# A tick's loads stand in the program behind its two sets, in place of ahead of them

## The chip, the core and the metric

The kernel runs on one core of a Trainium2 chip. The metric is device time in microseconds (us) of one execution. The program is written in Python and unrolled completely: every engine (PE for matmuls with PEld for its weight loads, DVE, ACT, POOL, and SP, which only issues DMAs here) gets its own list of instructions and works through it in the order in which the source emits them. A last pass (`keep_order`) ties each instruction to the one before it on its engine, so that the order of the source is the order of execution on every engine.

## What is computed

The input x is 8 images of 8 channels, 512 x 512, float32. Layer 0 normalizes groups of two channels and adds a spectral convolution of 4 x 4 modes. Layer 1 normalizes again (its result is called xn here) and then does this:

```python
drive = grid = xn
for _ in range(15):
    mapped = R * grid * (1.0 - grid)
    local = conv3x3_per_channel(mapped, K_local)
    grid = (1 - BETA) * ((1 - EPS) * mapped + EPS * local) + BETA * drive
cml = clip(grid, 0.0001, 1 - 0.0001)
nca = sigmoid(conv1x1(relu(conv3x3(xn, Wp, bp)), Wu, bu))        # 128 hidden channels
g = sigmoid(conv1x1(relu(conv3x3(concat(xn, cml, nca), Wg1, bg1)), Wg2, bg2))
out = x + g * cml + (1 - g) * nca
```

## The kernel before

**Elements and halves.** An element is one image (b = 0 to 7). The fifteen steps of an element are done in two halves of four channels each. A half keeps its grid in 5 tiles `m[k]` (k = 0 to 4), each of which holds four slabs of 32 rows. One *set* is one step of one tile: 96 matmul instructions into two PSUM pairs (`convolve`, L528), two DVE instructions that add the drive (`settle`, L583), and two squares on ACT (L589). A half has 75 sets, in the order of steps, and within a step of k. The drive comes in two layouts, dE for even steps and dO for odd ones, so a half needs 5 dE and 5 dO tiles as well.

**Ticks.** A tick, counted by t, does two sets, then up to two *hidden rounds* (L628 and the ReLU on ACT at L634 and on DVE at L636), then a gate or a piece of layer 0 of the next element, and, behind every second round, the 1 x 1 convolution of the hidden rounds (L647). An element has 75 ticks: its first half begins at t = 0, its second in the middle of tick 37. The hidden convolution of the next element and the gates of the previous element run beside the sets.

**Slots.** Work tiles live in slots. A `Slots` object is a first-in-first-out queue of free slots: `take` takes the one that came free first, `drop` appends one. A tile that is put into a slot waits, on the chip, for the last user of the tile that was there. `sets` has 15 slots, exactly what one half needs (5 m, 5 dE, 5 dO). The slots of dE and dO are dropped in `settle` at steps 14 and 15. The slot of m is dropped behind the store of its final grid (`leave`, the cml stores of L569), which is put off to the end of the tick. `shared` has 5 slots for gates (gin and mix, two slots a gate) and for the x tiles of layer 0.

**What a tick emits, in order.**
- `others.feed(t)`: loads of gates (six DMAs each, L683 and L688), when slots are free and at most one is loaded already; loads of x (L186). They go to SP.
- `prepare(n)` of each half in progress: n is the number of sets since that half's start, negative before it. For tile k, at n = k - 2 it takes a slot for m[k], POOL sets its edges (L507), and ACT squares dE into it (`square`, L508); at n = 2k - 5 POOL scales dO (`drive`, L521). From n = -11 on it also loads the half's dE and dO (four DMAs of 256 KB each, L491), as long as slots are free; also on SP.
- the two sets; between them `others.finish()`: the last DVE step of a gate (L726) and its out store (L733, on SP).
- the hidden rounds, with the load of the next cols tile behind every fourth (L611, on SP).
- the gate or layer 0 work; a gate is convolved (L698) in a later tick than the one in which it is loaded.
- `tick()`: what was put off. That is the exchange of halo rows between the m tiles (`renew`, L558), the cml stores (L569), the y store (L663), the store of xn (L417).

Before the first element come 8 rounds without sets, and behind the last one a tail that has only hidden rounds and gates; both go through the same `work`.

The lines that move:

```python
            while n >= -11 and self.loads and (self.loads[0][2] or sets.free):
                self.load(nc.sync)
```

## Time and profile before

| | |
|---|---|
| median of 3 runs | 10126.7 us (10123.93 to 10132.92) |
| the profiled execution | 10129.58 us, its span 10127.8 us |
| PE busy | 9436.5 us, 93% of the span |
| PEld, DVE, ACT, POOL busy | 4308.9, 5848.6, 4299.5, 1766.8 us |
| mean granted TensorE clock | 0.983 |
| moved by DMA | 1353.5 MB, 134 GB/s on average |

The span is the time from the first to the last instruction in one profiled execution. Busy times add up the instructions of an engine. In the lists of waits, "A <- B" means that A stood idle until B ended; "SPq" is the SP queue, and "issue" is idle time for which no semaphore is seen. In a timeline the columns are start in us, length in us, the engine and line, the operation, what it writes and reads, and how many were merged.

### The profile page before, as it was taken

What the parts mean: (1) busy time and instruction counts of PE and PEld (TensorE: products, weight loads), DVE (VectorE), ACT (ScalarE), POOL (GpSimd) and SP (SyncE); (2) the same over time, 40 slices, a digit from 0 to 9 for tenths busy, and PEclk for the clock granted to TensorE, in tenths of its full rate; (3) what the DMA queues carried; (4) which work ended last, traced back from release to release, by engine and by line L of the source; (5) the groups of instructions that cost most, each with busy time, mean ns of one, the idle gap of its engine ahead of it and who ended that gap; (6) DMA issues with size and microseconds to landing.
All of it is one profiled execution on the core that took longest, in us unless ns stands there. A gap on an engine that the chain in (4) does not pass through costs nothing. (4 is left out here: it accounts for less than half of the span.)

```text
span 10127.8 us, 353307 instructions
## 1 busy us (share of the span) xinstructions
PE 9436.5 (93%) x160496; PEld 4308.9 (43%) x160496; DVE 5848.6 (58%) x6067; ACT 4299.5 (42%) x4445; POOL 1766.8 (17%) x1406
## 2 busy tenths in 40 slices
PE   6998999999999999999999999999999999998999
PEld 3444444444444444444444444444444444444333
DVE  5654555755557555665555655566555665555555
ACT  2444444444444444444444444444444444444433
POOL 2010111202112021111211112111121201312212
PEclk9999999999999999999999999999999999999999
DMA  5231255535555465544555455554555535663578
GB/s 170 81 84 48 62 147 137 152 103 141 142 149 147 109 150 135 153 138 121 142 137 147 127 123 144 138 141 129 134 146 134 157 117 132 155 145 95 139 194 199
DMA packets 625565, 1353.50 MB, mean 134 GB/s; under 512 B 73067, under 2 KB 73195, under 8 KB 594051
## 3 DMA queue, kind: packets, MB, share of 16 engines
q1 hardware_dynamic: 621728, 1329.77, 50.7%
q8 instruction: 1261, 20.66, 0.9%
q14 instruction: 238, 1.94, 0.1%
q10 hardware_dynamic: 2338, 1.13, 0.0%
HBM read 992.27 MB, written 268.78 MB: 125 GB/s over the span
## 5 line engine op out<-in xcount | busy, mean ns | idle before, releaser
L528 PE MATMUL pair<-m,band 32*32 32x512 f32 x115200 | 4118.2, 608 | 177.2 <-issue 109.1
L589 ACT ACTIVATE m<-m 128x1024 f32<-128x1024 f32 x2240 | 2360.0, 1055 | 2811.5 <-DVE m L583 2695.1
L528 PEld LDWEIGHTS pair<-m,band 32*32 32x32 f32 x115200 | 2268.6, 104 | 1943.4 <-issue 1106.4
L628 PE MATMUL pair<-cols,w_p 32*128 32x511 f32 (+1 forms) x24576 | 2874.7, 605 | 42.8 <-issue 22.2
L583 DVE SCALAR_TENSOR_TENSOR m<-pair,dO 128x1024 f32<-128x1024 f32 x1280 | 1507.5, 1219 | 1372.5 <-PE pair L528 1176.3
L583 DVE SCALAR_TENSOR_TENSOR m<-pair,dE 128x1024 f32<-128x1024 f32 x1120 | 1319.7, 1220 | 1222.4 <-PE pair L528 1039.2
L628 PEld LDWEIGHTS pair<-cols,w_p 32*128 32x128 f32 x24576 | 1284.6, 187 | 1647.0 <-issue 1138.0
L636 DVE TENSOR_SCALAR h<-pair,b_p 128x1024 f32<-128x1024 f32 x1024 | 1313.5, 1283 | 838.7 <-PE pair L628 838.2
L634 ACT ACTIVATE h<-pair,b_p 128x1024 f32<-128x1024 f32 x1024 | 1140.7, 1114 | 990.0 <-PE pair L628 981.7
L721 POOL TENSOR_TENSOR mix<-mix 96x512 f32<-96x512 f32 x344 | 437.5, 1272 | 4413.2 <-ACT mix L719 4067.7
L647 PE MATMUL pair<-h,w_u 128*32 128x512 f32 x8192 | 1014.9, 606 | 205.4 <-DVE h L636 189.3
L698 PE MATMUL pair<-gin,w_g 128*32 128x511 f32 (+1 forms) x8256 | 965.7, 599 | 5.9 <-DMA mix<-xn 3.3
L703 POOL TENSOR_TENSOR mix<-mix 96x512 f32<-96x512 f32 x344 | 437.9, 1273 | 1420.7 <-DMA mix<-nca 1340.7
L593 POOL TENSOR_SCALAR dO<-dO 128x2048 f32<-128x2048 f32 x80 | 431.7, 5408 | 1263.2 <-DVE m L583 1263.1
L647 PEld LDWEIGHTS pair<-h,w_u 128*32 128x32 f32 x8192 | 254.3, 110 | 848.8 <-issue 367.6
L660 ACT ACTIVATE y<-y,b_u 128x512 f32<-128x512 f32 x256 | 184.8, 722 | 908.4 <-DVE y L656 908.4
L698 PEld LDWEIGHTS pair<-gin,w_g 128*32 128x32 f32 x8256 | 237.2, 110 | 681.6 <-issue 464.8
L715 PE MATMUL pair<-mix,w_g 128*32 128x512 f32 x2064 | 358.8, 595 | 85.2 <-DVE mix L708 85.2
L654 ACT COPY y<-pair 128x512 f32<-128x512 f32 x256 | 149.9, 585 | 631.1 <-PE pair L647 527.0
L708 DVE TENSOR_SCALAR mix<-pair,b_g 128x512 f32<-128x512 f32 x344 | 257.9, 750 | 254.2 <-PE pair L698 254.2
L726 DVE SCALAR_TENSOR_TENSOR mix<-mix,back 96x512 f32<-96x512 f32 x344 | 316.1, 919 | 150.8 <-POOL mix L721 150.8
L521 POOL TENSOR_SCALAR dO<-dO,base 128x512 f32<-128x512 f32 x320 | 226.8, 724 | 783.0 <-DMA dO<-xn 728.0
(85 smaller groups left out, 2642.2 us busy)
## 6 DMA issues: line engine op xcount, KB each, us to landing
gin<-xn SPq DMA_DIRECT2D x344, 384.0 KB
cols<-xn SPq DMA_DIRECT2D x256, 512.0 KB
x<-in_x SPq DMA_DIRECT2D x120, 1024.0 KB
gin<-cml SPq DMA_DIRECT2D x344, 320.0 KB
gin<-nca SPq DMA_DIRECT2D x344, 320.0 KB
dE<-xn SPq DMA_DIRECT2D x320, 256.0 KB
dO<-xn SPq DMA_DIRECT2D x320, 256.0 KB
mix<-xn SPq DMA_DIRECT2D x344, 192.0 KB
```

Source lines behind the costliest of these rows:

```text
L528: nc.tensor.matmul(ps[h // 2][32 * t : 32 * t + 32, h % 2], band[at, c0 + (t if step % 2 else h), dx], m[at, t, dx : dx + N], start=(n == ...
L583: nc.vector.scalar_tensor_tensor(u[:, at], ps[q], FLOOR, d[:, at], ALU.max, ALU.add)
L589: nc.scalar.square(u[:, at], u[:, at])
L593: nc.gpsimd.tensor_scalar(d, d, 0.5, None, ALU.add)
L628: nc.tensor.matmul(ps[g // 2][:, g % 2, lo:hi], w_p[p, dx, i % 2], self.cols[p, i // 2, at : at + hi - lo], start=(n == 0), stop=(n == 2), ...
L634: nc.scalar.activation(h[:, :2], ps[0], AF.Relu, bias=b_p)
L636: nc.vector.tensor_scalar(h[:, 2:], ps[1], b_p, 0.0, ALU.add, ALU.max)
L647: nc.tensor.matmul(ps[32 * g : 32 * g + 32], w_u[:, r % 4], h[:, g], start=(r == self.hs[0][0]), stop=(r == self.hs[-1][0]), tile_position ...
L698: nc.tensor.matmul(ps[32 * j : 32 * j + 32, lo:hi], gband[:, dx], gin[:, j, at : at + hi - lo], start=(n == 0), stop=(n == 2), tile_positi ...
L703: nc.gpsimd.tensor_tensor(d, d, ng, ALU.subtract)
L715: nc.tensor.matmul(ps[at], gpoint[:, at], mix[:, 3], start=True, stop=True, tile_position=(0, 32 * j),)
L721: nc.gpsimd.tensor_tensor(d, d, mix[: GR * C, 2], ALU.mult)
```

## The change

The loading loop leaves `prepare` and becomes a function of its own, `fetch`. A tick gathers its `feed` and the `fetch` of its halves in `transfers`, which `work` calls behind the two sets and behind `others.finish()`, ahead of the hidden rounds. The squares and drives of `prepare` stay where they were. The rounds ahead of the first element and the tail call theirs at the same place in `work`.

```diff
                 if 2 * k - 5 in (n, n + 1):
                     self.drive(k, 1)
+
+        def fetch(self, n):
             while n >= -11 and self.loads and (self.loads[0][2] or sets.free):
                 self.load(nc.sync)
...
-    def work(sets, rounds, e, after):
+    def work(sets, rounds, e, after, transfers):
...
         others.finish()
+        transfers()
         for ps in (pairs[:2], pairs[2:])[:rounds]:
             e.hidden.round(ps, after, settled)
...
-        work([], 2, e, None)
+        work([], 2, e, None, lambda: e.first.fetch(-11))
...
-            others.feed(t)
-            e.first.prepare(2 * t)
-            e.second.prepare(2 * t - TICKS)
+            halves = [(e.first, 2 * t), (e.second, 2 * t - TICKS)]
             if after:
-                after.first.prepare(2 * t - 2 * TICKS)
+                halves.append((after.first, 2 * t - 2 * TICKS))
+            for half, n in halves:
+                half.prepare(n)
+
+            def transfers():
+                others.feed(t)
+                for half, n in halves:
+                    half.fetch(n)
+
...
-            work(now_sets, min(more, 2 - e.hidden.n % 2), e, after and after.hidden)
+            work(now_sets, min(more, 2 - e.hidden.n % 2), e, after and after.hidden, transfers)
...
-        others.feed(TICKS)
-        work([], min(2, ROUNDS - e.hidden.n), e, None)
+        work([], min(2, ROUNDS - e.hidden.n), e, None, lambda: others.feed(TICKS))
```

## The prediction

> **What bounds the kernel now.** I read the page's busy shares and DMA queues (packets, MB, share), then the waits (us in total, times, longest us), then the timelines of single ticks.

> ```profile
> PE 9436.5 (93%) x160496; PEld 4308.9 (43%) x160496; DVE 5848.6 (58%) x6067; ACT 4299.5 (42%) x4445; POOL 1766.8 (17%) x1406
> q8 instruction: 1261, 20.66, 0.9%
> ```

> ```profile
> PE pair L528 <- issue: 109.1, 65, 4.5
> POOL m L507 <- DMA cml<-m: 114.2, 12, 16.5
> ACT m L508 <- POOL m L507: 44.2, 10, 12.4
> SPq L491 <- DMA cml<-m: 47.3, 51, 2.4
> ```

> TensorE is busy for 93% of the span, and no wait of PE names a load for more than 14.2 us in total. So a load's place can matter in two ways only: it makes TensorE wait through another engine, or it slows TensorE's own instruction stream. The four waits show both. "issue" is a PE gap that no semaphore explains. The next two are the squares (L508) that wait for a memset (L507), which waits until the store of a finished set has freed its slot. The last is the same wait, borne by the SP queue for loads, where it costs nothing.

> Where a square has this wait, this follows (timeline of ACT and POOL, then windows of three ticks; columns are length, PE, PEld, DVE, ACT, POOL busy, then the clock):

> ```profile
> 775.01 0.11 POOL L507 MEMSET m<- 128x8 f32 x1 [16.55 <-DMA cml<-m]
> 775.16 2.00 ACT L508 ACTIVATE m<-dE,mhalf 128x2048 f32<-128x2048 f32 x1 [9.72 <-POOL m L507]
> 777.06 2.93 ACT L589 ACTIVATE m<-m 128x1024 f32<-128x1024 f32 x3
> 779.90 1.09 ACT L634 ACTIVATE h<-pair,b_p 128x1024 f32<-128x1024 f32 x1
> ...
> 746.30:762.00 15.70, 14.22 (x264) 6.85 (x264) 8.41 (x7) 8.61 (x7) 8.79 (x11) 1.00 0.91 252
> 762.00:784.90 22.90, 16.40 (x266) 5.82 (x265) 7.97 (x7) 10.40 (x9) 9.89 (x9) 0.83 0.56 144
> ```

> The squares of the sets and the hidden rounds' L634 stand behind L508 on ACT; PE's L647 needs L634. The tick takes 22.9 us in place of 15.7, and the clock falls to 0.83.

> [...] 17% of 22.9 us = 3.9 us lost to the clock behind a 6.4 us gap. [...] 322,961 PE records / 256 = 1261.6, and q8 has 1261 packets. [...] every issue gap over 1 us ends at a record whose number has the same remainder by 256 (193), and a q8 packet began 2.2 to 3.2 us earlier. [...] the trace shows fetches 3 to 6 us late while gate loads are outstanding and within 1.5 us when nothing is.

> **The change, part by part.**

> Instructions: none is added or removed. All that is moved are DMA issues on SP (gate loads L683 and L688, x loads L186, set loads L491); feed and fetch issue nothing on other engines. Squares, memsets and drives stay at the head. In the SP queue the loads pass only the out store (L733) of the same tick; the cols loads, renewals (L558) and cml stores (L569) stay behind them.

> (a) Gate and x loads, later. A typical tick starts at 5318.5:

> ```profile
> 5320.57 0.38 SPq L663 DMA_DIRECT2D nca<-y  x1
> 5321.05 0.38 SPq L683 DMA_DIRECT2D gin<-xn  x1
> ...
> 5324.33 0.42 SPq L688 DMA_DIRECT2D mix<-nca  x1
> 5324.96 0.85 SPq L733 DMA_DIRECT2D out<-mix  x1
> ```

> The out store waits for DVE's L726 and goes out 6.45 us into the tick in nearly every gate tick. The six loads will follow it, at 7.3 to 10 in place of 2.5 to 6, about 5 us later on average. The gate's convolution comes in the next tick; from the landing of gin (judged by the queue's later waits) to L698 there are 18 us in the median now, so this costs nothing but some 8 us in the last element, whose ticks are 11 to 14 us and whose renewals have 2 to 12 us of slack. In the tail the last gates' loads stand behind an out store: 3 us.

> (b) A gain from the same shift. The sets occupy PE for the first 6.6 us of a tick, where 256 instructions pass in 4.4 us; behind them they take 8 to 11. So only a fetch asked for in the first 3 us stalls PE, and the gate loads go out just then. Issue gaps sum to 133 us (all lines), 85 of them in ticks with gate loads. About 20 of these are in ticks without an out store (the two-gate starts, t = 2 and 51), where nothing moves. Of the other 65 I take half as gained, 33: the shifted loads land until 18 us, that is, into the head of the next tick. Clock lost behind such gaps is 0.6 us for 1 us of gap (32 windows of 3.4 us at half speed behind 92 us of gaps), 20 more. The bounds are 0 and 104. In the hand-over ticks (c) the loads leave the head too: 10.

> (c) Slots handed over at a half's end. This is the largest part, and it is a matter of which slot goes to whom. Free slots form a queue. At the end of a half the slots of dE and dO come free in settle, those of m only after their cml store. Now a tick's squares are served first, from what earlier ticks freed. They take the d slots (the waits of L507 for "DVE m L583", 61 times), and the loads take the m slots and wait on SP. Only the fifth square of each half gets an m slot: the 12 waits above. With fetch behind the sets, the loads take the d slots in the tick that frees them. The next tick's squares find m slots alone. By hand, with n counted to the new half's start, and a slot named by the set of the old half (0 to 74) that frees it (m70 is the grid of set 70, d70 its drive): second halves give square 0 slot m70 (tick n = -3), squares 1 and 2 m72 and m73 (n = -1), square 3 d74, square 4 m74; first halves give squares 0 and 1 m71 and m72 (n = -2), squares 2 and 3 d74 and m73. The stores of m72 and m73 were issued at the end of the tick just before. So **a wait moves from SP to POOL and ACT**.

> Its price in a second half (SP timeline; the tick with n = -1 starts at 6879.9):

> ```profile
> 6864.59 1.77 SPq L491 DMA_DIRECT2D dO<-xn  x4
> 6866.40 1.85 SPq L491 DMA_DIRECT2D dE<-xn  x4
> 6868.76 4.08 SPq L491 DMA_DIRECT2D dO<-xn  x4
> 6873.73 8.08 SPq L569 DMA_DIRECT2D cml<-m  x8
> 6883.89 2.44 SPq L491 DMA_DIRECT2D dE<-xn  x4
> 6886.51 1.70 SPq L491 DMA_DIRECT2D dO<-xn  x4
> ```

> The last two loads show when the stores of m72 and m73 have landed: 6883.9 and 6886.5. The twelve loads ahead of the stores start at 6864.6 now. In the new order the first of them takes m71's slot, and m71's store itself stands behind eight loads that leave 5 us later. I reckon the first load at 6872, so the stores land 7 to 8 us later, the last at 6894.5. Then: square 2.0, L589 1.06, L634 1.11, L589 1.05, L634 1.11 = 6900.8; PE is at L647 at 6894.3 now: 6.5 lost. In the other five of elements 1 to 6 the store lands 0.6 to 4.6 us later in its tick; the six sum to 49. Element 0 (m73 lands at 760.5, L647 at 760.1): 14. Element 7 (m73 at about 9215.8): 18. Square 0 in the short ticks of elements 0 and 7: 9.

> First halves, seven: m72 lands at 4996.5 in the tick from 4986.6; no L589 stands between, so 4996.5 + 6 + 2.0 + 2.2 = 5006.7 against L647 at 5001.5: 5.2 each, 36.

> Clock: 15 gaps of 5 to 18 us at about 3 us: 45. Given back: the fifth square's store no longer stands behind loads: 7 in element 0, 12 in element 7, 1 in the others: 25. Sum: 49 + 14 + 18 + 9 + 36 + 45 - 25 = 146. Bounds: with no later landing the gaps of first halves vanish and 10 to 20 stays; with 3 us more it is 200.

> **Sum.** 146 + 8 + 3 - 33 - 20 - 10 = +94. The profiled execution took 10129.6 (span 10127.8), so 10223.6 by its own time; it stands 2.9 above the median, so 10221.

> **Rivals.**

> Faster: the fetches decide. The store of m72 lands no later than now (the DMA queue drains faster than I reckon), L508 then ends before L634 is due, and (b) brings its full 104 + 10. Against it: the 12 waits already there cost 7 us in element 0. Price: 20 + 11 - 114 = -83, 10044. It decides where the landing slips by less than about 3 us, half of what I reckon. Chance 0.10.

> No change: slip and fetches cancel, or SP trails so far that the loads' place is idle (in the tick from 5015.5 the gate loads already go out 6.5 us in). 10127. Chance 0.10.

> Slower, more: the shifted loads also push renewals and gate loads past their use in the last element's short ticks, 10 ticks by 4 us: 10261. Chance 0.12. My forecast has 0.68.

> So faster 0.10, within 0.2% (some 20 us, about what a measurement of this kernel can tell from no change) 0.10, slower 0.80. The range 10120 to 10285 takes in the cancelling case and the dearer one, and leaves the faster one out.

> **What would show it.** Right: the waits of L507 for cml stores rise from 12 to some 60 and those of L508 for L507 to over 150 us; "PE L647 <- ACT h L634" grows from 14 us to about 100, at 15 hand-overs; gate loads follow the out store; PE's issue gaps fall to about 90. Wrong: L508 without waits, or issue gaps near 20 with an unchanged L647.

## The result, and the profile after

The changed kernel takes 10068.3 us (median of 5 runs, 10056.9 to 10083.9), the kernel before 10126.7 us beside it. The ratio is 0.9947, 95% interval 0.9934 to 0.996: **faster by 0.5%**, where the prediction had it slower by 0.9%. The profiled execution has a span of 10066.0 us in place of 10127.8, so 61.8 us are to be found in the trace.

In the changed kernel's line numbers everything from `fetch` on stands two further down (L530 for L528, L509 and L510 for the memset and the square, L636 for L634). The page's lines of TensorE and the instruction queue, then rows of the waits (us in total, times, longest us), two of before and four of after:

```profile
PE 9398.8 (93%) x160496; PEld 4288.8 (43%) x160496; DVE 5870.8 (58%) x6067; ACT 4301.6 (43%) x4445; POOL 1764.5 (18%) x1406
q8 instruction: 1261, 20.66, 0.9%
```

```profile
PE pair L628 <- issue: 22.2, 16, 4.1
PE pair L647 <- ACT h L634: 14.2, 32, 6.4
```

```profile
PE pair L530 <- issue: 87.8, 65, 3.9
PE pair L649 <- ACT h L636: 23.8, 35, 9.8
POOL m L509 <- DMA cml<-m: 330.1, 27, 16.1
ACT m L510 <- POOL m L509: 116.0, 27, 15.3
```

The same work is done by the same number of instructions. The waits of the squares have grown as forecast: those of the memset for a store from 114 to 330 us, those of the square for the memset from 44 to 116. What did not come is their price: TensorE's wait for L636 grows by 10 us, from 14.2 to 23.8, not to about 100. And TensorE's unexplained gaps shrink: within the ticks they sum to 132.9 us before and 96.9 after.

**One tick shows where the time came from.** It is tick 58 of element 4. Its TensorE before, then after (start, length, instructions, and in brackets the idle time before them with what ended it):

```profile
5970.14 6.51 PE L528 MATMUL pair<-m,band 32*32 32x512 f32 x185
5979.80 1.93 PE L528 MATMUL pair<-m,band 32*32 32x512 f32 x7 [3.15 <-issue]
5981.66 7.44 PE L628 MATMUL pair<-cols,w_p 32*128 32x512 f32 x48
```

```profile
5918.05 6.58 PE L530 MATMUL pair<-m,band 32*32 32x512 f32 x192
5924.56 5.43 PE L630 MATMUL pair<-cols,w_p 32*128 32x512 f32 x48
```

Before, TensorE stops 7 instructions short of the sets' end, waits 3.15 us for no semaphore, and goes on slowly: the hidden rounds take 7.44 us in place of 5.43. SP's queue in the same tick, before and after (of six gate loads, the first and the last):

```profile
5968.82 0.35 SPq L683 DMA_DIRECT2D gin<-xn  x1
...
5970.96 0.42 SPq L688 DMA_DIRECT2D mix<-nca  x1
5976.58 0.86 SPq L733 DMA_DIRECT2D out<-mix  x1
```

```profile
5924.50 0.83 SPq L735 DMA_DIRECT2D out<-mix  x1
5925.44 0.82 SPq L685 DMA_DIRECT2D gin<-xn  x1
...
5928.10 0.92 SPq L690 DMA_DIRECT2D mix<-nca  x1
```

Before, six loads (1600 KB) go out around the tick's start; after, they follow the out store, 7.4 to 10 us into the tick. The windows of this tick, before and after (columns as in the prediction):

```profile
5970.14:5994.31 24.17, 21.02 (x290) 8.50 (x287) 10.03 (x10) 7.03 (x7) 2.51 (x2) 0.86 0.40 96
```

```profile
5918.05:5935.20 17.15, 17.15 (x290) 7.76 (x287) 10.03 (x10) 7.03 (x7) 2.56 (x2) 1.00 0.61 128
```

The same 290 matmuls and the same work on DVE and ACT take 24.17 us before and 17.15 after: 3.15 us of stall and 14% of the clock, 3.4 us, make 6.5 of the 7.0.

**The whole span, by kind of tick.** Each cell is the sum of tick lengths and, behind the stroke, of TensorE's issue gaps over 0.15 us, worked out from the traces. Gate ticks are t = 2 to 26 and 51 to 72 of elements 1 to 6; the hand-overs are t = 73 to 1 (second half to the next element's first) and t = 34 to 39 (first half to second).

| us / us of issue gaps | ticks | before | after | difference |
|---|---|---|---|---|
| gate ticks | 282 | 4778.9 / 83.1 | 4681.9 / 37.4 | -97.0 |
| hand-over second to first | 28 | 390.8 / 9.0 | 419.6 / 18.3 | +28.8 |
| hand-over first to second | 48 | 803.0 / 28.2 | 785.4 / 19.1 | -17.6 |
| rest of element 7 | 66 | 811.9 / 8.1 | 835.1 / 19.9 | +23.2 |
| rest of element 0, other ticks | 175 | 2676.8 / 4.5 | 2673.7 / 2.3 | -3.1 |
| ahead of the first tick, and tail | | 666.4 | 670.4 | +3.9 |

Clock lost in gate ticks falls from 46.1 to 10.2 us. With the 45.7 us of gaps that makes 81.6 of the 97.0; the other 15 are in neither. So the gain is larger than the result shows: what the hand-overs from second to first half and element 7 lose, 52 us, is over half of what the gate ticks gain.

### The profile page after: what moved, and what is told of

It is laid out like the page before. It is cut to its first block, busy times and chain, and to the rows that moved or that the text cites. A ratio compares the mean times of both kernels' runs of the same rounds, so it can differ in the third digit from the quotient of the medians.

```text
span 10066.0 us, 353339 instructions
## 1 busy us (share of the span) xinstructions
PE 9398.8 (93%) x160496; PEld 4288.8 (43%) x160496; DVE 5870.8 (58%) x6067; ACT 4301.6 (43%) x4445; POOL 1764.5 (18%) x1406
## 3 DMA queue, kind: packets, MB, share of 16 engines
q8 instruction: 1261, 20.66, 0.9%
## 5 line engine op out<-in xcount | busy, mean ns | idle before, releaser
L530 PE MATMUL pair<-m,band 32*32 32x512 f32 x115200 | 4123.9, 609 | 158.6 <-issue 87.8
L530 PEld LDWEIGHTS pair<-m,band 32*32 32x32 f32 x115200 | 2264.3, 104 | 1936.8 <-issue 1125.0
L630 PE MATMUL pair<-cols,w_p 32*128 32x511 f32 (+1 forms) x24576 | 2841.0, 601 | 30.4 <-DMA cols<-xn 14.4
L638 DVE TENSOR_SCALAR h<-pair,b_p 128x1024 f32<-128x1024 f32 x1024 | 1313.4, 1283 | 788.1 <-PE pair L630 787.1
L636 ACT ACTIVATE h<-pair,b_p 128x1024 f32<-128x1024 f32 x1024 | 1141.4, 1115 | 888.1 <-PE pair L630 875.0
L700 PE MATMUL pair<-gin,w_g 128*32 128x511 f32 (+1 forms) x8256 | 960.4, 598 | 9.5 <-DMA gin<-nca 3.6
L700 PEld LDWEIGHTS pair<-gin,w_g 128*32 128x32 f32 x8256 | 234.6, 109 | 683.8 <-issue 466.5
L728 DVE SCALAR_TENSOR_TENSOR mix<-mix,back 96x512 f32<-96x512 f32 x344 | 334.0, 971 | 150.8 <-POOL mix L723 150.8
L721 ACT ACTIVATE mix<-pair,b_g 96x512 f32<-96x512 f32 x344 | 233.0, 677 | 278.1 <-PE pair L717 184.0
```

The source lines that it names most:

```text
L530: nc.tensor.matmul(ps[h // 2][32 * t : 32 * t + 32, h % 2], band[at, c0 + (t if step % 2 else h), dx], m[at, t, dx : dx + N], start=(n == ...
L630: nc.tensor.matmul(ps[g // 2][:, g % 2, lo:hi], w_p[p, dx, i % 2], self.cols[p, i // 2, at : at + hi - lo], start=(n == 0), stop=(n == 2), ...
L636: nc.scalar.activation(h[:, :2], ps[0], AF.Relu, bias=b_p)
L638: nc.vector.tensor_scalar(h[:, 2:], ps[1], b_p, 0.0, ALU.add, ALU.max)
L700: nc.tensor.matmul(ps[32 * j : 32 * j + 32, lo:hi], gband[:, dx], gin[:, j, at : at + hi - lo], start=(n == 0), stop=(n == 2), tile_positi ...
```

## The experiments

Theory F: the gain is TensorE's instruction fetch (the packets of q8), and what counts is which DMAs are outstanding (issued and not yet landed) in the first microseconds of a tick. Theory S: it comes from the set loads and their slots. Theory Q: from the order in SP's queue. All ratios are against the kernel before on the same chip.

**Gate and x loads alone.** The set loads go back ahead of the sets (in this run and in those built on it, the loads of the opening go back to the head of their rounds too):

```diff
                 half.prepare(n)
+                half.fetch(n)
 
             def transfers():
                 others.feed(t)
-                for half, n in halves:
-                    half.fetch(n)
```

> The gate and x loads stand behind the two sets as in the changed kernel; the loads of dE and dO stay ahead of them as in the kernel before. Theory F (the gain is TensorE's instruction fetch, which no longer meets gate loads in the head of a tick): the gate ticks of elements 1 to 6 (t = 2 to 26 and 51 to 72) shorten as in the changed kernel, by 80 to 97 us, with their issue gaps near 37 us in place of 83; the hand-over from second to first half (t = 73 to 1) keeps the 391 us of before in place of 420; in all 10030 to 10060 us, faster than the changed kernel. Theory S (the gain comes from the set loads and the slots that they take): no change against before, 10120 to 10135, issue gaps in gate ticks near 80.

Measured: 10056.7 us, ratio 0.9938 (0.9925 to 0.9951). Gate ticks 4678.9 us with 37.1 us of issue gaps; the hand-over is back at 391.9. Moving the gate loads alone brings the whole gain. By the intervals it can't be told from the changed kernel, so that part of the expectation stays open; its profiled span, 10046.9 us, is 19 us shorter, but it is the fastest of its five runs.

**Set loads alone.** The mirror image:

```diff
+            others.feed(t)
             for half, n in halves:
                 half.prepare(n)
 
             def transfers():
-                others.feed(t)
                 for half, n in halves:
                     half.fetch(n)
```

> Only the loads of dE and dO stand behind the sets; gate and x loads stay ahead of them. Theory F: gate ticks keep their issue gaps (about 83 us) and length (4779 us); the hand-overs from second to first half take 415 to 425 us in place of 391, those from first to second 785 to 803; in all 10125 to 10160 us, not faster than before. Theory S: 10060 to 10080 us, the changed kernel's time.

Measured: 10138.4 us, ratio 1.0016 (1.0008 to 1.0025). Gate ticks 4782.8 / 90.5; hand-over second to first 424.5, first to second 788.1. Theory S falls: this half of the change costs 13 us by the medians, 8 to 25 by the interval.

**The gate loads later still**: the kernel with the gate loads alone moved, and these behind the hidden rounds:

```diff
         others.finish()
-        transfers()
         for ps in (pairs[:2], pairs[2:])[:rounds]:
             e.hidden.round(ps, after, settled)
         next(settled, None)
+        transfers()
```

> As with the gate loads alone moved, but they stand behind the hidden rounds too, so that they go out at 13 us of a tick or later and are outstanding in the first 5 us of the next. Theory F: it is not being behind the sets that counts but what is outstanding in the first 3 us of a tick: issue gaps in the gate ticks return to 70 us or more, time 10090 to 10170. Rival theory Q (the gain is SP's queue, in which something else had stood behind the gate loads): as fast as with the gate loads behind the sets, issue gaps near 37.

Measured: 10215.3 us, ratio 1.0091 (1.0074 to 1.0107), beyond the expected range. A wait of TensorE and a tick's SP queue (this tick starts at 5317.54 and ends at 5334.68):

```profile
PE pair L530 <- issue: 157.6, 105, 3.9
```

```profile
5329.56 0.39 SPq L613 DMA_DIRECT2D cols<-xn  x1
5330.05 0.41 SPq L685 DMA_DIRECT2D gin<-xn  x1
...
5332.51 0.42 SPq L690 DMA_DIRECT2D mix<-nca  x1
```

The loads leave 12.5 to 15 us into this tick, the last of them 2.2 us before the next begins. From the mean rate of this run's span, 133 GB/s, I estimate 12 us for their 1600 KB, so they are still under way in the next head. Gate ticks take 4829.9 us with 103.0 of issue gaps, more than before. So "later" is no gain in itself: of the three places, only 7.4 to 9.8 us into a tick (the median with these loads right behind the sets) has gained.

**Between the two sets**, ahead of the out store; otherwise as with the gate loads alone moved:

```diff
             next(settled)
+            if transfers:
+                transfers()
+            transfers = None
             others.finish()
         others.finish()
-        transfers()
+        if transfers:
+            transfers()
```

> The kernel with the gate loads alone moved, but they stand between the two sets, ahead of the out store (L733). SP runs ahead of TensorE, so without the out store's wait in front of them the loads should go out in the first 6 us of a tick as in the kernel before. Theory F: what counts is the time at which they go out, so issue gaps in gate ticks near 83 us and 10110 to 10145 us. Rival theory P (any place behind the first set will do): issue gaps under 50, time under 10080.

Measured: 10129.5 us, ratio 1.0004 (0.9992 to 1.0016); gate ticks 4789.0 / 91.4. The SP queue around a tick that starts at 5292.94:

```profile
5291.97 0.64 SPq L690 DMA_DIRECT2D mix<-nca  x1
5299.38 0.86 SPq L735 DMA_DIRECT2D out<-mix  x1
```

The loads stand behind a set in the program and yet go out ahead of it. In gate ticks the first and the last of them leave 2.5 and 5.3 us into a tick in the median, the same as in the kernel before (7.4 and 9.8 with the gate loads behind both sets), and nothing is gained. SP sent these loads as early as its waits let it. It is the out store's wait for DVE (in the changed kernel 273 waits of L735 for L728, 1482.5 us) that puts the loads behind the sets in time as well.

**Other traffic.** To the kernel with the gate loads alone moved are added six idle DMAs of 256 KB. In the program they stand at the head of the tick after each gate load:

```diff
                 g.load()
+                self.extra += 1
...
+            for i in range(6 * others.extra):
+                nc.sync.dma_start(
+                    out=view(spare[i % 12], 0, [[N, P], [1, N]]),
+                    in_=view(e.xn, 16 * i * C * N, [[N, P], [1, N]]),
+                )
+            others.extra = 0
```

> The kernel with the gate loads alone behind the sets, plus six idle DMAs of 256 KB each (from xn to a spare place in HBM that nobody reads) at the head of the tick after each gate load. Theory F: whatever moves in the first 3 us of a tick makes the fetch late: issue gaps in gate ticks go from 37 us back to 75 us or more, gate ticks from 4679 to 4750 or more, time 10110 to 10250, with no wait of PE for a DMA grown by more than 10 us. Rival theory Q (it was the place of the gate loads in SP's queue): issue gaps stay under 50 and the time within 20 us of 10057.

Measured: 10516.9 us, ratio 1.0385 (1.0368 to 1.0402): 460 us above the kernel without them, where at most 193 were expected. Its waits of TensorE:

```profile
PE pair L530 <- issue: 217.1, 117, 4.5
...
PE pair L700 <- DMA gin<-nca: 105.9, 33, 9.3
```

Issue gaps in gate ticks go from 37 to 196 us, and the clock lost there from 6.8 to 97.3. Of the 336 us that gate ticks grow by, the gaps are 158 and the clock 90. The second row was not expected: the traffic also delays gate loads, mostly in element 7.

The figures contradict Q, which had under 50 us of gaps. But the run is not the clean case that was meant. The idle DMAs did not keep to the head, and the gate loads kept their place in the program only, as SP's queue shows for a tick from 5309.04 to 5327.80:

```profile
5314.82 8.68 SPq L935 DMA_DIRECT2D spare<-xn  x6
5323.60 0.87 SPq L735 DMA_DIRECT2D out<-mix  x1
5324.58 0.44 SPq L685 DMA_DIRECT2D gin<-xn  x1
```

SP trailed behind. In gate ticks the first idle DMA leaves 7.2 us into a tick in the median, and the first gate load 12.3 in place of 7.4, as late as with the gate loads behind the hidden rounds (12.1), so that by the same estimate gate loads reach into the next head too. That more traffic means more stalls is shown, and the gaps are nearly double those of that kernel (103); how much of it the idle bytes did, and how much the later gate loads, is not.

**The instructions shifted.** In the kernel before, 64 small matmuls are repeated in the opening:

```diff
-            for h in range(2):
+            for h in [0, 1] * (17 if e.b == 0 and c == 0 else 1):
```

> The kernel before with 64 matmuls of layer 0's first tile repeated on TensorE (16 columns each, in the opening in which TensorE waits for x), so every later instruction stands 128 records further on. Theory F: TensorE stalls where a block of 256 records ends, whatever instruction stands there. Every issue gap over 1 us still ends at a record number with remainder 193 by 256, so at another matmul; fewer than a third of the ticks with such a gap are the same as before; their sum can be anything from 60 to 190 us in place of 133, and the time moves with it by about 1.5 us for 1 us of gap: 10060 to 10220. Theory I (the stalls belong to certain instructions or ticks of the program): the same ticks stall, the sum stays within 10 us, the time at 10127 to 10133.

Measured: 10127.6 us, ratio 1.0003 (0.9994 to 1.0012). All 53 issue gaps over 1 us still end at a record number with remainder 193 or 194 by 256, as all 56 within the ticks before, so now 128 records earlier in the program's own work. (Records are TensorE's weight loads, 160496 before, its matmuls, as many, and 1969 instructions of its sequencer, counted together.) That the gaps belong to blocks of 256 is shown. But 28 of the 53 ticks that stall are the same as before, not fewer than a third. The kernel with the set loads alone moved, whose blocks lie as before, shares 36 of its 53. So the shift of the blocks changes less than was thought; that the loads of a tick settle the rest is argued here, not shown. The sum is 146.5 us against 132.9, and the time fits both theories: the alignment was no lever for the total.

**Slots kept for the squares.** The changed kernel, in which loads leave the next tick's squares their slots:

```diff
-            while n >= -11 and self.loads and (self.loads[0][2] or sets.free):
+            kept = sum(k - 2 in (n + 2, n + 3) for k in range(SETS))
+            while n >= -11 and self.loads and (self.loads[0][2] or len(sets.free) > kept):
```

> The changed kernel, but the set loads leave as many free slots as the next tick's squares will take, so that squares get the slots of dE and dO again and the loads those that wait for a cml store. Theory C (the changed kernel's longer hand-over from second to first half is its squares' wait for stores): the hand-over falls from 420 to 400 us or less, waits of L508 for L509 from 116 to under 50 us, time 10040 to 10060. Theory F alone (it is fetch stalls of loads and stores in the head): hand-over stays at 410 to 425 us, time 10060 to 10080.

Measured: 10038.9 us, ratio 0.991 (0.9895 to 0.9925). The wait of the squares in its trace (its lines stand one further down):

```profile
ACT m L511 <- POOL m L510: 6.9, 1, 6.9
```

The squares' wait is gone, and with it TensorE's gaps with a named cause at these hand-overs: 30.4 us, as before, against 37.0 in the changed kernel. The hand-over takes 406.1 us, between the two expectations: its issue gaps stay at 18.3. So both causes are in the 28.8 us that the hand-over had lost. The profiled execution, with a span of 10059.9 us, is the longest of six; the rest of what the median gained is not located.

**The parts put together.** Gate and x loads behind the sets in elements 0 to 6, ahead of them in element 7; set loads of second halves behind the sets, those of first halves ahead of them:

```diff
                 half.prepare(n)
-                half.fetch(n)
+                if half is not e.second:
+                    half.fetch(n)
+            if not after:
+                others.feed(t)
 
             def transfers():
-                others.feed(t)
+                if after:
+                    others.feed(t)
+                e.second.fetch(2 * t - TICKS)
```

(against the kernel with the gate loads alone moved)

> The parts put together as the regions of the earlier runs suggest: gate and x loads behind the sets in elements 0 to 6 and ahead of them in element 7; set loads of second halves behind the sets, those of first halves ahead of them. If the regions add up (gate ticks 4680 us, hand-over second to first 391, first to second 786, rest of element 7 812): about 10056 - 19 - 17 = 10020 us, 10005 to 10040. If the fetch stalls only move from one region to another: 10050 or more.

Measured: **10015.0 us, ratio 0.9889 (0.9871 to 0.9906)**. The regions add up: gate ticks 4668.4 / 32.4, hand-over second to first 392.7, first to second 794.0 (8 more than hoped), rest of element 7 803.6 / 5.0. This version beats both kernels.

The gate ticks of the ten traces have 2167 blocks that begin in the first 3 us of a tick, the stretch that theory F names. In 1051 cases fewer than 8 packets of the data queue were under way on average over the next 3 us, and no stall over 1 us followed. In 1116 cases there were 8 or more, and 274 stalls followed. The kernel before has 131 of its 218 such blocks in the second group, with 31 stalls; the changed kernel has 70 of 216, with 10; the one with idle traffic has 168 of 220, with 73. This is a count and not an experiment of its own, but it shows block by block what theory F says of the whole.

## Why the prediction was wrong

Both paths were in the text, and the wrong one was taken for the larger: "the fetches decide", the rival that was given 0.10 and 10044 us, is what happened. The forecast fell because step (c) was priced at 136 us (146, less the 10 of the hand-over ticks), and the net of the hand-overs is 11. Of the 156 us between +94 and the profiled -61.8, this makes 125. The gate ticks gained 44 more than reckoned, and element 7 and the tail lost 15 more.

**Step (c), the failed one.** Two of its terms were wrong. The first is *"I reckon the first load at 6872, so the stores land 7 to 8 us later"*. That is 10.3 us into a tick from 6861.7. The same stretch of SP after the change, in ticks from 6785.31 and 6802.15:

```profile
6789.89 2.05 SPq L491 DMA_DIRECT2D dE<-xn  x4
6792.42 2.22 SPq L491 DMA_DIRECT2D dO<-xn  x4
6795.15 3.95 SPq L491 DMA_DIRECT2D dE<-xn  x4
6799.91 7.79 SPq L571 DMA_DIRECT2D cml<-m  x8
```

The first load leaves 4.6 us into its tick: it takes the slot of m70, not of m71, and waits only 1.0 us for that store. It left at 2.9 before, so the slip is 1.7. The last of the two stores (m73) lands 10.6 us into the next tick, about 4 later than before, where 14.6 was reckoned. And this half is among the worst: over the 15 hand-overs the stores of tiles 1 to 3 land about 0.8 us later on average (from 1.7 earlier to 4.5 later). The rival's own point of decision was "less than about 3 us".

The second is who waits. I gave slots of m to squares 0, 1, 2 and 4 of a second half and to squares 0, 1 and 3 of a first half. That follows from "the loads take the d slots in the tick that frees them", and this holds for the first of a tick's two sets alone. The `settle` of the second set ends in the hidden rounds, behind `fetch`, so its d slot is still there for the next tick's squares. Followed through the program in this way, the queue gives slots of m to squares 2 and 4 of a second half and to 1, 3 and 4 of a first half. The trace agrees: squares 1 and 3 wait in first halves, square 2 (and 4, in six of eight) in second ones, so the memset's waits for stores come to 27 in place of some 60. ACT and POOL show what such a wait costs:

```profile
6810.26 0.11 POOL L509 MEMSET m<- 128x8 f32 x1 [14.29 <-DMA cml<-m]
```

```profile
6810.40 2.01 ACT L510 ACTIVATE m<-dE,mhalf 128x2048 f32<-128x2048 f32 x1 [6.89 <-POOL m L509]
6812.31 1.03 ACT L591 ACTIVATE m<-m 128x1024 f32<-128x1024 f32 x1
6813.26 1.09 ACT L636 ACTIVATE h<-pair,b_p 128x1024 f32<-128x1024 f32 x1
...
6815.20 1.10 ACT L636 ACTIVATE h<-pair,b_p 128x1024 f32<-128x1024 f32 x1
```

The square starts 8.2 us into the tick and is done 10.2 us into it, just when the ReLU's turn comes. The second L636 ends at 14.15 us of the tick. Before, the tick started at 6879.95, and its second L634 was this one:

```profile
6892.71 1.11 ACT L634 ACTIVATE h<-pair,b_p 128x1024 f32<-128x1024 f32 x1 [0.51 <-PE pair L628]
```

It ended at 13.87: 0.3 us lost, not 6.5. ACT's wait lies in slack, and the step counted as lost what only used the slack up. The lower bound that the text gave for this step, "with no later landing [...] 10 to 20 stays", is near what came: TensorE's gaps with a named cause grew by 8.5 us in the two kinds of hand-over together (79.1 to 87.6). Its condition holds only nearly, since the stores do land later.

What the second-to-first hand-over does lose, 28.8 us, was not in the prediction: TensorE's gaps with a named cause grow by 6.6, the others are issue gaps (9.3 more) and clock (13.7, none before). In tick 0 of element 2:

```profile
2511.93 6.53 PE L530 MATMUL pair<-m,band 32*32 32x512 f32 x187
2520.55 1.05 PE L530 MATMUL pair<-m,band 32*32 32x512 f32 x5 [2.09 <-issue]
```

Six cml stores go out here from 0.6 to 6.7 us into the tick, where there were four until 4.6: the moved loads pushed stores into the head. From first to second half the loads leave the head as was said, and the 17.6 us gained there are mostly issue gaps (9.1 fewer) and clock (7.2 less).

**Step (b), right in kind, too small.** Within the ticks issue gaps of 132.9 us fell to 96.9; "about 90" was said. They end at record numbers with remainder 193 or 194, not 193 alone. Nor is it only a fetch asked for in the first 3 us of a tick that stalls TensorE: of the 56 gaps over 1 us within the ticks before, 47 follow a block that begins there, 9 one that begins 3.9 to 15.6 us into the tick. But the total hides several movements. The gate ticks lost 45.7 us of gaps (33 reckoned, half of 65) and 35.9 of clock (20 reckoned), and shortened by 97. The bound of 104 was nearer than the middle. The reason given for taking half, that shifted loads land until 18 us and so in the next head, may hold in part: 37 us of gaps remain.

**Step (a), too small, and in part by another cause.** Element 7 lost 23 us where 8 were reckoned, half of it by issue gaps (8.1 to 19.9) and 3.4 by the clock: its ticks take 12.4 us in the median, its gate loads leave at 9.0 in place of 3.8, and in the head of the tick there is more traffic, on average 9.0 packets of the data queue under way in the first 3 us in place of 4.6. Put back ahead of the sets there, the 66 ticks take 804 us. The tail lost 2.8; 3 was said. From gin's landing to the gate's convolution the median is now 10.7 us in place of 17.9, which still costs next to nothing: TensorE waits 3.6 us in all for gin at L700.

Over all ticks the issue gaps sum to 133 us before and 97 after, to 70 in the best version and to 256 with the idle traffic.

## What to carry to other kernels

In this kernel DMAs that TensorE does not wait for cost it time. At the head of a tick it runs through its instructions fastest (in tick 58 after the change, 192 matmuls in 6.6 us and the other 98 in 10.6), and there its own fetch came late when much else was under way (no stall over 1 us in 1051 cases with under 8 packets under way, 274 in 1116 with more). So read "issue" gaps, see whether their record numbers share a remainder, and try the bulk loads in the part of the loop in which instructions are fewer: behind the sets the gate ticks took 97 us less. On SP's queue, which runs ahead here, it was a wait that put them there (the first at 7.4 us of a tick); behind one set, without that wait, they left at 2.5 us and the ratio was 1.0004. And before a new wait on a feeding engine is priced as loss, subtract the slack that stands behind it: here the waits grew by 72 us on ACT and by 10 on TensorE.

## What was not expected of the hardware

- Gaps of one to four microseconds came with nearly as much again in clock: in gate ticks, 45.7 us fewer gaps came with 35.9 us less lost to the clock. In the kernel before, the clock fell to half speed during 21 of the 25 issue gaps over 2 us (the longest was 4.5) or within 3 us behind them, and so it did at 6 of the 32 between 1 and 2 us. Of the 69 stretches at half speed within its ticks, 42 lasted 3.4 us, 24 lasted 6.8 and 3 lasted 10.2.
- A load that nobody needs cost TensorE more than the bytes suggest. Six idle DMAs a gate, 1.5 MB, raised the issue gaps in gate ticks from 37 to 196 us, partly by pushing the gate loads later; the gate's own 1600 KB at the head of the tick make them 83. Why the effect is so large is not shown.
